# Making the table of q: order of the constants, size of the statistics' parts, and which engine normalises

## The chip, the cores and the metric

The kernel runs on one core of one Trainium2 chip. A core has five engines that each work through their own list of instructions in order and wait for each other through semaphores: PE (matrix products and transposes), DVE (VectorE), ACT (ScalarE), POOL (GpSimd) and SP (SyncE, which here issues DMAs). Sixteen DMA engines move data between the main memory and the core's SBUF. The metric is the device time of one execution in microseconds (us), as the median of several. All times below are us unless they say otherwise.

## What is computed

One layer of a graph network on 12,500 nodes and 212,500 edges, sorted by their target `dst`; a node has 128 features in 8 heads of 16. `x` are the nodes' features, `edge_attr` the edges', and `k`, `v` and `q` are linear maps with weights and biases:

```python
h = jnp.maximum(_layernorm(x), 0.0)
q = (h @ Wq.T + bq).reshape(N, 8, 16)
k = (edge_attr @ Wk.T + bk).reshape(-1, 8, 16)
v = (h @ Wv.T + bv).reshape(N, 8, 16)
qs, qd = q[src], q[dst]
in_m, out_m, diag_m = sum(qs * k), sum(qd * k), sum(qs * qd)   # over the 16 of a head
score = (softmax_by_dst(in_m / 4) + softmax_by_dst(out_m / 4)
         + softmax_by_dst(diag_m / 4)) * weight ** lam
out = segment_sum(score * v[dst], dst) @ Wo.T + bo
return x + leaky_relu(out, 0.1)
```

`_layernorm` subtracts a node's mean over its 128 features and divides by the root of its variance plus 1e-5. The change lies in the first two lines: normalise, cut at zero, multiply by Wq.

## The kernel before, in words

`ordered_path` does the work when `dst` is sorted, which it checks on the way; `general_path` is there for other inputs and is not entered. `ordered_path` has a preparation and then a loop over the edges.

**The preparation** (lines 676 to 984) makes two tables in main memory: `q_table`, q in fp32, one row of 512 bytes a node; and `q3_table`, the same numbers split in three bf16 terms. It also turns the lists of edges. The 12,500 nodes are 98 tiles of 128 nodes, which lie in `xq` [128, 98, 128] in SBUF; four tiles are a group `g`, so there are 25 groups (GN), the last of two tiles. For a group there are these steps:

- `statistics(lo, hi)` (L832 to L847): on DVE one `bn_stats` a tile (L836), then five small operations on a whole part (L841 to L846) that make the sum and the square deviation of each node. Parts are those of the loads of x: 4, 4, 6 and then 14 tiles at a time.
- `scale` (L849 to L854): a root on ACT (L851), a reciprocal (L852) and a product (L853) on DVE, which give each node's factor `inv` and summand `shift`.
- `rectify(g)` (L862 to L865): ACT normalises each of the four tiles in place and cuts at zero in the same pass (L864, 128x128).
- `turn_h(g)` (L867 to L873): PE turns the four tiles into `h_ps` (L871), ACT copies them to `hT` (L873, 128x512).
- `nodes_q(g)` (L875 to L885): PE multiplies by Wq into `q_ps` (L879), DVE adds the bias and writes q over the group's tiles in `xq` (L882), SP writes them to `q_table` (L883).

These are staggered: the loop `for g in range(-2, GN)` issues `rectify(g + 2)`, `turn_h(g + 1)` and `nodes_q(g)`, then `ready` (the scales that will be needed) and `measure` (statistics up to 6 to 12 groups ahead). `h_ps` and `q_ps` have three buffers each.

Beside that loop runs other preparation, hung on it by a table `side` that names a step g: `edges_0` (POOL turns the indices `src_r` and `dst_r` into floats, L778 and L779), `turn_ws` (three weights), `biases`, `edges_1` (PE turns the sources, sixteen transposes into four buffers of `t_ps`, L765, and DVE copies them to `src_i`, L766; then POOL takes differences of neighbours in dst, `step`, L784), `edges_2` (the same turning for the edges' weights into `att_t`) and `edges_3` (POOL makes the segments' borders, L791, DVE makes dst relative, L796, POOL casts it, L799). `t_ps` has two buffers. `step` lies in the memory of `src_r`, so it waits until the sources are turned.

**What sets the order.** Nearly every instruction is passed through `pin`, which chains it behind the one pinned before it on its engine: the program's order is the engine's order. The framework adds the waits for data. The DMAs that SP issues share eight semaphores in turn, so each waits until the eighth before it has landed. SP's list, in order: lam, Wq, the loads of x (ten, L688 and L690), src, weight and dst (L602 to L604), three biases, then sixteen DMAs that pick single indices out of dst (`bases`, `heads`, `tops`, L731 to L738; 83 or 84 numbers of 4 bytes each but the last), then the 25 writes of `q_table` (L883), among them, behind the seventh, three writes of the biases' terms (L828) and, behind the tenth, the fetch of the edges' features of step 0 (`ea`, L643, 1280 KB) and two of single indices, then the borders and relative targets (L803 to L805) and the 25 writes of `q3_table` (L905).

After the loop over g, POOL issues 50 gathers: `gather(0)` to `gather(11)`, four DMAs each, and two for the 20 odd edges (L651, L674). A gather fetches 128 rows of `q_table` by the indices in `src_i`; it needs all of `q_table` written. Beside them ACT and DVE make the terms of q3 (`terms_q`, L896 to L903), with four buffers.

**The loop over edges** (L1377, 415 blocks of 512 edges in 83 steps of five) turns the edges' features, multiplies them by Wk, spreads the targets' q by a one-hot product from `q3_table`, multiplies with the gathered rows, sums over heads, and does the three softmaxes by scans. Its working memory lies where the preparation's was, so its first instructions wait for what used that.

Of the kernel before, what the change touches and what calls it, by code (L numbers as in the profile page):

```python
# [7 lines left out]
F32 = mybir.dt.float32  # L8
# [464 lines left out]
def ordered_path(ctx: ExitStack, tc: tile.TileContext, flag, x, src, dst, edge_attr, edge_weight,  # L473
# [66 lines left out]


    consts = ctx.enter_context(tc.tile_pool(name="consts", bufs=1))
    jp = consts.tile([P, P], I32, name="jp")
    nc.gpsimd.iota(jp, pattern=[[1, P]], base=0, channel_multiplier=-1)
    ident = consts.tile([P, P], F32, name="ident")
    nc.vector.tensor_scalar(ident, jp, 0.0, None, op0=ALU.is_equal)

    third = consts.tile([P, 1], F32, name="third")
    threes = consts.tile([P, W], F32, name="threes")
# [8 lines left out]

    eps = consts.tile([P, 1], F32, name="eps")
    nc.vector.memset(eps, EPS)  # L560
    wq, wv, wk, wo = [consts.tile([P, F], F32, name=n) for n in ("wq", "wv", "wk", "wo")]
# [24 lines left out]
    load = edges.enter_context(tc.tile_pool(name="load", bufs=2))  # L586

    pinned = {}

    def pin(inst):  # L590

        engine = str(inst.ins.engine)
        if engine in pinned:
            tc.add_manual_dep(inst.ins, pinned[engine], mybir.DependencyInfo(
                mybir.DependencyClass.NoSync, mybir.DependencyReason.DATA), reason="in order")
        pinned[engine] = inst.ins.name
        return inst

# [93 lines left out]
    with tc.tile_pool(name="prep", bufs=1) as prep, \  # L692
# [67 lines left out]
        def turn_edges(of, to, which=range(RB)):  # L760
            cols = of.rearrange("r (a p j) -> r a j p", a=RB, j=JN)
            for a in which:
                t_ps = prep_ps.tile([P, JN, RW], F32, name="t_ps")
                for j in range(JN):
                    pin(nc.tensor.transpose(t_ps[:, j, :], cols[:, a, j, :], ident[:RW, :RW]))  # L765
                pin(nc.vector.tensor_copy(to[:, a:NB:RB, :], t_ps.rearrange("p j r -> p r j")))  # L766
# [9 lines left out]
        def edges_0():  # L776

            pin(nc.gpsimd.tensor_copy(src_f, src_r))  # L778
            pin(nc.gpsimd.tensor_copy(dst_f, dst_r))  # L779

        def edges_1():
            turn_edges(src_f, src_i)
            step = got["step"] = prep.tile([RW, RC + 1], F32, name="step", tag="step")
            pin(nc.gpsimd.tensor_sub(step, dst_f[:, 1:], dst_f[:, :RC + 1]))  # L784

        def edges_2():
            turn_edges(weight, att_t)

# [41 lines left out]

        def statistics(lo, hi):

            n = hi - lo
            stats = node.tile([P, CH, 6], F32, name="stats", bufs=1)[:, :n]
            for i in range(n):
                pin(nc.vector.bn_stats(stats[:, i, :], xq[:, lo + i, :]))  # L836


            sums3 = node.tile([P, 3, CH], F32, name="sums3", bufs=4)[:, :, :n]
            total, apart, sq = sums3[:, 0], sums3[:, 1], sums3[:, 2]  # L840
            pin(nc.vector.tensor_add(total, stats[:, :, 1], stats[:, :, 4]))  # L841
            pin(nc.vector.tensor_sub(apart, stats[:, :, 1], stats[:, :, 4]))
            pin(nc.vector.tensor_add(sq, stats[:, :, 2], stats[:, :, 5]))
            pin(nc.vector.scalar_tensor_tensor(apart, apart, F / 4.0, apart, op0=ALU.mult,
                                               op1=ALU.mult))
            pin(nc.vector.tensor_add(sq, sq, apart))  # L846
            return lo, hi, total, sq  # L847
# [14 lines left out]
        def rectify(g):  # L862
            for i in tiles_of(g):
                pin(nc.scalar.activation(xq[:, i, :], xq[:, i, :], AF.Relu, bias=shift[:, i:i + 1],  # L864
                                         scale=inv[:, i:i + 1]))  # L865

        def turn_h(g):  # L867
            n = len(tiles_of(g))
            h_ps = node_ps.tile([P, JN, P], F32, name="h_ps")
            for b, i in enumerate(tiles_of(g)):  # L870
                pin(nc.tensor.transpose(h_ps[:, b, :], xq[:, i, :], ident))  # L871
            hT = hTs[g] = node.tile([P, JN, P], F32, name="hT", bufs=2)
            pin(nc.scalar.copy(hT[:, :n], h_ps[:, :n]))  # L873

# [33 lines left out]

        side = {0: edges_0, 4: turn_ws, 6: biases, 9: edges_1, 15: edges_2, 18: edges_3}
        turn_w(0, wq)  # L910
        parts = [(2 * lo, 2 * hi) for lo, hi in zip(LOADS, LOADS[1:])]

        measured = []

        def measure(upto):

            while parts and parts[0][0] < (upto + 1) * JN:
                measured.append(statistics(*parts.pop(0)))

        def ready(upto):  # L920
# [606 lines left out]
```

## Time and profile before

| what | value |
| --- | --- |
| median of 10 runs | 2692.48 (2686.34 to 2695.48) |
| the profiled execution | 2694.61 |
| its span, first to last instruction | 2692.8 |
| granted PE clock, mean | 0.754 |
| busy in the span: PE, DVE, ACT, POOL | 1773.1, 2001.5, 1342.6, 1644.9 |
| moved by DMA | 351.19 MB, 130 GB/s over the span |

The preparation and the start of the loop in stretches of 10 us, busy time of each engine and what the DMA did:

| us | PE | DVE | ACT | POOL | DMA share | GB/s |
| --- | --- | --- | --- | --- | --- | --- |
| 10 to 20 | 7.19 | 7.53 | 8.01 | 3.70 | 1.10 | 345 |
| 20 to 30 | 8.64 | 8.68 | 8.56 | 0.33 | 1.07 | 263 |
| 30 to 40 | 7.72 | 9.86 | 8.94 | 1.92 | 0.51 | 121 |
| 40 to 50 | 1.69 | 9.76 | 3.11 | 1.90 | 0.07 | 1 |
| 50 to 60 | 9.65 | 4.92 | 7.26 | 7.98 | 0.70 | 232 |
| 60 to 70 | 9.43 | 5.57 | 9.38 | 2.74 | 1.01 | 327 |
| 70 to 80 | 9.13 | 5.51 | 9.66 | 3.94 | 0.45 | 154 |
| 80 to 90 | 1.45 | 8.50 | 4.44 | 5.44 | 0.90 | 277 |
| 100 to 110 | 0.00 | 7.92 | 6.94 | 7.60 | 0.71 | 241 |

How to read it: a span in the profile runs from the first to the last instruction of one execution. A row of the timeline gives the start, the duration, the engine, the line, the operation and its tiles (out<-in); what stands in square brackets is how long the engine had been idle and what ended that. `SPq` rows are the issue of a DMA, not its transfer. A row with xN holds N instructions that followed each other, and its duration is from the first's start to the last's end. In rows of stretches each engine has its busy time and number of instructions, then the granted PE clock, the DMA's share and its GB/s.

### The profile page before, as it was taken

To read this page: it belongs to the slowest core of one execution; us is meant where nothing else is said; L and a number is where in the kernel's file an instruction comes from. 1 tells how busy PE (TensorE), PEld (TensorE's weight loads), DVE (VectorE), ACT (ScalarE), POOL (GpSimd) and SP (SyncE) were. 2 spreads that over 40 slices of the span, in tenths; PEclk is the share of its full clock that TensorE was granted. 3 is DMA by queue.
4 is the path that set the end of the run, shared out by engine and by line. 5 is a ranking of instruction groups with operands and counts; after the bars stand their busy time and mean duration, and the time that the engine had idled before them with its cause. 6 is when DMAs were issued, how large, how long until landed. Compare 5 with 4: busy or idle time off the path is not lost.

```text
span 2692.8 us, 34795 instructions
## 1 busy us (share of the span) xinstructions
PE 1773.1 (66%) x10209; PEld 1430.8 (53%) x10209; DVE 2001.5 (74%) x2582; ACT 1342.6 (50%) x2445; POOL 1644.9 (61%) x1690
## 2 busy tenths in 40 slices
PE   6136665667576676776766677677766676667775
PEld 5135454545465564555655565565555555555654
DVE  7547777777687777777777777787777777778784
ACT  6534444445455454554545455445454555445572
POOL 4656666666666666666666666666666666666610
PEclk9667778777767767787777777766787778777687
DMA  7764334444444444434444444444444444444431
GB/s 206 229 199 136 113 113 132 120 120 114 139 126 123 117 140 132 124 116 146 126 121 124 142 131 119 124 138 131 118 120 141 130 123 123 137 130 125 117 100 52
DMA packets 314459, 351.19 MB, mean 130 GB/s; under 512 B 132882, under 2 KB 234013, under 8 KB 313952
## 3 DMA queue, kind: packets, MB, share of 16 engines
q1 hardware_dynamic: 245493, 233.57, 27.4%
q0 software_dynamic: 53344, 109.11, 16.2%
q10 hardware_dynamic: 15424, 6.19, 0.9%
q8 instruction: 83, 1.36, 0.2%
q14 instruction: 115, 0.94, 0.1%
HBM read 316.50 MB, written 32.17 MB: 129 GB/s over the span
## 4 chain that ended last, share of the span: by engine, by line
PE 26%; ACT 11%; another core or an unknown queue 11%; issue 9%; DVE 9%; DMA 1%; POOL 0%; SPq 0%; DVEq 0%; ACTq 0%; POOLq 0%
PE k_ps L1127 9%; PE w_ps L1274 5%; PE eT_ps L1118 3%; PE qd_ps L1135 3%; ACT eT L1120 2%; DVE u L1202 2%; ACT relb L1112 2%; PE k_ps L1125 2%; ACT qd L1138 2%; ACT sel L1264 1%; ACT oh L1113 1%; DVE prod L1146 1%; ACT sel L1263 1%; DVE prod L1147 1%
## 5 line engine op out<-in xcount | busy, mean ns | idle before, releaser
L651 POOL DMA_INDIRECT qq<-q_table,src_i x1660 | 1609.6, 970 | 883.8 <-issue 359.4
L1127 PE MATMUL k_ps<-wk,eT 128*128 128x128 f32 x3320 | 659.5, 360 | 594.4 <-ACT eT L1120 363.4
L1127 PEld LDWEIGHTS k_ps<-wk,eT 128*128 128x128 f32 x3320 | 559.7, 255 | 750.9 <-ACT eT L1120 420.7
L1149 DVE TENSOR_REDUCE lT<-prod 128x96 f32<-128x1536 f32 x415 | 727.5, 1753 | 14.3
L1120 ACT COPY eT<-eT_ps 128x512 f32<-128x512 f32 x415 | 243.7, 587 | 910.5 <-remote 626.8
L1146 DVE TENSOR_TENSOR prod<-qd,k_ps 128x512 f32<-128x512 f32 x415 | 280.8, 677 | 169.6 <-remote 79.0
L1118 PE MATMUL eT_ps<-ident,ea 128*128 128x128 f32 x1660 | 343.6, 346 | 1.0 <-DVE found L956 1.0
L1135 PE MATMUL qd_ps<-win,oh 126*128 126x128 bf16 x1660 | 190.4, 246 | 199.6 <-DMA q_table<-q 72.1
L1138 ACT COPY qd<-qd_ps 128x512 f32<-128x512 f32 x415 | 239.4, 577 | 125.3 <-remote 32.0
L1112 ACT ACTIVATE relb<-relb,before 126x512 bf16<-126x512 bf16 x415 | 301.6, 727 | 0.0
L1147 DVE TENSOR_TENSOR prod<-qq,qd_ps 128x512 f32<-128x512 f32 x415 | 281.9, 679 | 0.0
L1148 DVE TENSOR_TENSOR prod<-qq,k_ps 128x512 f32<-128x512 f32 x415 | 281.8, 679 | 0.0
L1135 PEld LDWEIGHTS <-oh 126*128 126x128 bf16 x1660 | 148.1, 112 | 250.8 <-issue 168.1
L1113 ACT ACTIVATE oh<-relb 126x512 bf16<-126x512 bf16 x415 | 261.4, 630 | 34.2 <-issue 21.0
L1118 PEld LDWEIGHTS eT_ps<-ident,ea 128*128 128x128 f32 x1660 | 276.0, 184 | 1.3 <-DVE found L956 1.3
L1202 DVE TENSOR_TENSOR_SCAN u<-far,u,l_ps 120x512 f32<-120x512 bf16 x82 | 104.9, 1279 | 230.4 <-remote 57.3
L1274 PE MATMUL w_ps<-back,sel 128*126 128x144 f32 (+1 forms) x1344 | 230.4, 334 | 29.5 <-ACT sel L1264 19.0
L1274 PEld LDWEIGHTS w_ps<-back,sel 128*126 128x126 f32 (+1 forms) x1344 | 212.5, 228 | 54.8 <-ACT sel L1264 43.9
L1125 PE MATMUL k_ps<-b,ones 3*128 3x512 bf16 x415 | 181.4, 437 | 18.9 <-DVE prod L1148 9.4
L1234 DVE TENSOR_TENSOR back<-lT,m_ps 128x480 f32<-128x480 f32 x83 | 54.0, 651 | 145.8 <-PE m_ps L1226 83.8
L1214 DVE TENSOR_TENSOR_SCAN m<-far,head,u 120x512 f32<-120x512 bf16 x83 | 106.4, 1282 | 0.1
L1279 ACT COPY rows<-w_ps 126x288 f32<-126x288 f32 x84 | 33.1, 394 | 122.9 <-PE qd_ps L1135 48.8
(192 smaller groups left out, 1390.9 us busy)
## 6 DMA issues: line engine op xcount, KB each, us to landing
ea<-in_edge_attr_dram SPq DMA_DIRECT2D x83, 1280.0 KB
relb<-rel_d SPq DMA_DIRECT2D x83, 630.0 KB
qq<-q_table,src_i POOLq DMA_INDIRECT x1660
win<-q_table SPq DMA_DIRECT2D x415, 31.5 KB
far<-far_d SPq DMA_DIRECT2D x84, 120.2 KB
q_table<-q SPq DMA_DIRECT2D x24, 384.0 KB
sums<-rows SPq DMA_DIRECT2D x412, 7.9 KB
q_table<-xq SPq DMA_DIRECT2D x24, 256.0 KB
```

The lines of the kernel that those rows point to most:

```text
L651: rows = pin(nc.gpsimd.indirect_dma_start(out=qq[:, j, :], out_offset=None, in_=q_table, in_offset=bass.IndirectOffsetOnAxis(ap=src_i[:, g ...
L1112: pin(nc.scalar.activation(d, d, AF.Abs, bias=before[:K3]))
L1113: pin(nc.scalar.activation(oh, d, AF.Relu, bias=1.0, scale=-1.0))
L1118: pin(nc.tensor.transpose(eT_ps[:, j, :], eas[g // S][:, g % S, j * F:(j + 1) * F], ident))
L1120: pin(nc.scalar.copy(eT, eT_ps))
L1127: pin(nc.tensor.matmul(k_ps[:, j, :], eTs[g][:, j, :], wk, start=False, stop=(j == JN - 1)))
L1135: pin(nc.tensor.matmul(qd_ps[:, j, :], ohs[g][:, j * P:(j + 1) * P], d["win"][:, s, :], start=(j == 0), stop=(j == JN - 1)))
L1138: pin(nc.scalar.copy(qds[g], qd_ps))
L1146: pin(nc.vector.tensor_mul(prod[:, :, 2, :], qds[g], ks[g]))
L1147: pin(nc.vector.tensor_mul(prod[:, :, 1, :], qqs[g], q_ps[g]))
L1149: pin(nc.vector.tensor_reduce(lTs[t][:, :, s, :], prod.rearrange("p j i (h d) -> p j (i h) d", d=DIM), AX.X, ALU.add))
L1274: pin(nc.tensor.matmul(w_ps[:, i].rearrange("p s c -> p (s c)"), d["sel"][:n, j, lo:lo + 3, :].rearrange("p s w -> p (s w)"), d["back"][:n ...
```

## The change

It does five things.

1. The identity matrix, the constant eps and one root of it (`root`, used by nobody) are pinned at the head of DVE's and ACT's lists.
2. The statistics go by parts of 4, 4, 8, 8, ..., 8, 2 tiles. `measure(n)` issues the next n `bn_stats`, whatever parts they lie in: eight before the loop, then six a step. When a part is full its five small operations follow; from tile 16 on they are six and run on POOL.
3. `rectify` no longer cuts at zero: `Relu` moves from the normalisation to the copy of `hT`. In the groups 3 to 11 the fourth tile is normalised by POOL (9 tiles), from group 12 on the third and fourth by DVE (24 tiles); the rest stays on ACT.
4. The table `side` is spread out: the sources' four pieces go at the steps 11, 12, 13 and 14, the weights' two halves at 15 and 16, and `edges_0` moves from step 0 to 9.
5. `measure` is called ahead of `ready` in a step instead of behind it, and `ready` looks three groups ahead instead of four.

The definition of `pin` moves up unchanged. The line numbers of the text are those of the kernel before.

```diff
--- before.py
+++ after.py
@@ -539,12 +539,27 @@
     sums = [dram.tile([NP, 2, 2 * H3], F32, name=f"sums{i}") for i in range(S)]
 
 
...
     consts = ctx.enter_context(tc.tile_pool(name="consts", bufs=1))
     jp = consts.tile([P, P], I32, name="jp")
     nc.gpsimd.iota(jp, pattern=[[1, P]], base=0, channel_multiplier=-1)
     ident = consts.tile([P, P], F32, name="ident")
-    nc.vector.tensor_scalar(ident, jp, 0.0, None, op0=ALU.is_equal)
-
+    pin(nc.vector.tensor_scalar(ident, jp, 0.0, None, op0=ALU.is_equal))
+
+    eps = consts.tile([P, 1], F32, name="eps")
+    pin(nc.vector.memset(eps, EPS))
+    root = consts.tile([P, 1], F32, name="root")
+    pin(nc.scalar.activation(root, eps, AF.Sqrt))
     third = consts.tile([P, 1], F32, name="third")
     threes = consts.tile([P, W], F32, name="threes")
     nc.gpsimd.iota(threes, pattern=[[3, W]], base=0, channel_multiplier=-1,
@@ -556,8 +571,6 @@
     ones3 = consts.tile([3, P], BF, name="ones3")
     nc.vector.memset(ones3, 1.0)
 
-    eps = consts.tile([P, 1], F32, name="eps")
-    nc.vector.memset(eps, EPS)
     wq, wv, wk, wo = [consts.tile([P, F], F32, name=n) for n in ("wq", "wv", "wk", "wo")]
     b3 = consts.tile([3, 3, F], BF, name="b3")
     bv3, bk3, bo3 = [b3[:, i, None, :].to_broadcast([3, JN, F]) for i in range(3)]
@@ -778,13 +780,28 @@
             pin(nc.gpsimd.tensor_copy(src_f, src_r))
             pin(nc.gpsimd.tensor_copy(dst_f, dst_r))
 
+        def turn_src(a):
+            turn_edges(src_f, src_i, [a])
+
         def edges_1():
-            turn_edges(src_f, src_i)
+            turn_src(3)
             step = got["step"] = prep.tile([RW, RC + 1], F32, name="step", tag="step")
             pin(nc.gpsimd.tensor_sub(step, dst_f[:, 1:], dst_f[:, :RC + 1]))
 
+        def edges_1a():
+            turn_src(0)
+
+        def edges_1b():
+            turn_src(1)
+
+        def edges_1c():
+            turn_src(2)
+
         def edges_2():
-            turn_edges(weight, att_t)
+            turn_edges(weight, att_t, (0, 1))
+
+        def edges_2b():
+            turn_edges(weight, att_t, (2, 3))
 
         def edges_3():
             of = got["cuts"] = of_tile()
@@ -828,22 +845,36 @@
                 pin(nc.sync.dma_start(b3[i:i + 1], terms[:, i]))
 
 
-        def statistics(lo, hi):
+        parts = [(0, 4), (4, 8)] + [(lo, min(lo + 8, NI)) for lo in range(8, NI, 8)]
+        waiting = [(lo, hi, i) for lo, hi in parts for i in range(lo, hi)]
+        measured, now = [], {}
+
+        def measure(n):
+
+            for lo, hi, i in waiting[:n]:
+                if i == lo:
+                    now["stats"] = node.tile([P, 8, 6], F32, name="stats", bufs=2)
+                pin(nc.vector.bn_stats(now["stats"][:, i - lo, :], xq[:, i, :]))
+                if i == hi - 1:
+                    measured.append(sum_up(lo, hi, now["stats"][:, :hi - lo]))
+            del waiting[:n]
+
+        def sum_up(lo, hi, stats):
 
             n = hi - lo
-            stats = node.tile([P, CH, 6], F32, name="stats", bufs=1)[:, :n]
-            for i in range(n):
-                pin(nc.vector.bn_stats(stats[:, i, :], xq[:, lo + i, :]))
-
-
-            sums3 = node.tile([P, 3, CH], F32, name="sums3", bufs=4)[:, :, :n]
-            total, apart, sq = sums3[:, 0], sums3[:, 1], sums3[:, 2]
-            pin(nc.vector.tensor_add(total, stats[:, :, 1], stats[:, :, 4]))
-            pin(nc.vector.tensor_sub(apart, stats[:, :, 1], stats[:, :, 4]))
-            pin(nc.vector.tensor_add(sq, stats[:, :, 2], stats[:, :, 5]))
-            pin(nc.vector.scalar_tensor_tensor(apart, apart, F / 4.0, apart, op0=ALU.mult,
-                                               op1=ALU.mult))
-            pin(nc.vector.tensor_add(sq, sq, apart))
+            sums2 = node.tile([P, 2, 8], F32, name="sums2", bufs=5)[:, :, :n]
+            total, sq = sums2[:, 0], sums2[:, 1]
+            apart = node.tile([P, 8], F32, name="apart", bufs=2)[:, :n]
+            of = nc.vector if lo < 16 else nc.gpsimd
+            pin(of.tensor_sub(apart, stats[:, :, 1], stats[:, :, 4]))
+            pin(of.tensor_add(sq, stats[:, :, 2], stats[:, :, 5]))
+            if lo < 16:
+                pin(of.scalar_tensor_tensor(apart, apart, F / 4.0, apart, op0=ALU.mult, op1=ALU.mult))
+            else:
+                pin(of.tensor_mul(apart, apart, apart))
+                pin(of.tensor_scalar(apart, apart, F / 4.0, None, op0=ALU.mult))
+            pin(of.tensor_add(sq, sq, apart))
+            pin(of.tensor_add(total, stats[:, :, 1], stats[:, :, 4]))
             return lo, hi, total, sq
 
         def scale(lo, hi, total, sq):
@@ -861,8 +892,14 @@
 
         def rectify(g):
             for i in tiles_of(g):
-                pin(nc.scalar.activation(xq[:, i, :], xq[:, i, :], AF.Relu, bias=shift[:, i:i + 1],
-                                         scale=inv[:, i:i + 1]))
+                aside = nc.gpsimd if 3 <= g < 12 and i % 4 == 3 else \
+                    nc.vector if g >= 12 and i % 4 > 1 else None
+                if aside:
+                    pin(aside.tensor_scalar(xq[:, i, :], xq[:, i, :], inv[:, i:i + 1],
+                                            shift[:, i:i + 1], op0=ALU.mult, op1=ALU.add))
+                else:
+                    pin(nc.scalar.activation(xq[:, i, :], xq[:, i, :], AF.Identity,
+                                             bias=shift[:, i:i + 1], scale=inv[:, i:i + 1]))
 
         def turn_h(g):
             n = len(tiles_of(g))
@@ -870,7 +907,7 @@
             for b, i in enumerate(tiles_of(g)):
                 pin(nc.tensor.transpose(h_ps[:, b, :], xq[:, i, :], ident))
             hT = hTs[g] = node.tile([P, JN, P], F32, name="hT", bufs=2)
-            pin(nc.scalar.copy(hT[:, :n], h_ps[:, :n]))
+            pin(nc.scalar.activation(hT[:, :n], h_ps[:, :n], AF.Relu))
 
         def nodes_q(g):
             n = len(tiles_of(g))
@@ -906,24 +943,16 @@
                     q3_table[3 * lo:3 * (lo + n * P), :].rearrange("(u p k) f -> p u (k f)", p=P, k=6),
                     q3.rearrange("p (u k) t f -> p u (k t f)", k=2)))
 
-        side = {0: edges_0, 4: turn_ws, 6: biases, 9: edges_1, 15: edges_2, 18: edges_3}
+        side = {4: turn_ws, 7: biases, 9: edges_0, 11: edges_1a, 12: edges_1b, 13: edges_1c, 14: edges_1,
+                15: edges_2, 16: edges_2b, 17: edges_3}
         turn_w(0, wq)
-        parts = [(2 * lo, 2 * hi) for lo, hi in zip(LOADS, LOADS[1:])]
-
-        measured = []
-
-        def measure(upto):
-
-            while parts and parts[0][0] < (upto + 1) * JN:
-                measured.append(statistics(*parts.pop(0)))
-
         def ready(upto):
 
             while measured and measured[0][0] < (upto + 1) * JN:
                 scale(*measured.pop(0))
 
-        measure(1)
-        ready(1)
+        measure(8)
+        ready(0)
         for g in range(-2, GN):
             if g + 2 < GN:
                 rectify(g + 2)
@@ -931,8 +960,8 @@
                 turn_h(g + 1)
             if g >= 0:
                 nodes_q(g)
-            ready(g + 4)
-            measure(g + 6 + min(max(g, 0), 6))
+            measure(6)
+            ready(g + 3)
             if g in side:
                 side[g]()
             if g == 9:
```

More of the change, by code (lines that the diff above doesn't have):

```diff
@@ L539, in ordered_path, with pin @@
     sums = [dram.tile([NP, 2, 2 * H3], F32, name=f"sums{i}") for i in range(S)]
+    pinned = {}
+    def pin(inst):
+        engine = str(inst.ins.engine)
+        if engine in pinned:
+            tc.add_manual_dep(inst.ins, pinned[engine], mybir.DependencyInfo(
+                mybir.DependencyClass.NoSync, mybir.DependencyReason.DATA), reason="in order")
+        pinned[engine] = inst.ins.name
+        return inst
     consts = ctx.enter_context(tc.tile_pool(name="consts", bufs=1))
@@ L586, in ordered_path @@
     load = edges.enter_context(tc.tile_pool(name="load", bufs=2))
[L588 to L597, printed above, removed]
     def rows_in(to, t, q):
```

## The prediction

> **What bounds the kernel now.** I read the page first, for its slices and its chain that ended last, then busy time in stretches of 2 us for the first 90 us, then the timeline of that start, engine by engine, then the rows of SP's queue and of the tile q_table.
>
> ```profile
> span 2692.8 us, 34795 instructions
> ...
> PE 26%; ACT 11%; another core or an unknown queue 11%; issue 9%; DVE 9%; DMA 1%; POOL 0%; SPq 0%; DVEq 0%; ACTq 0%; POOLq 0%
> ```
>
> The chain lies almost wholly in the loop over edges, which begins near 158 us. The change touches only what lies before 84 us, so the question is one shift: how much earlier does the loop begin? Its order on every engine is the same in both kernels. From the timeline of the start:
>
> ```profile
> 34.44 1.88 DVE L843 TENSOR_TENSOR sums<-stats 128x14 f32<-128x14 f32 x1
> ...
> 49.52 0.61 SPq L738 DMA_DIRECT2D tops<-in_dst_dram  x1
> 50.09 1.34 PEld L765 LDWEIGHTS t_ps<-ident,src_r 104*128 104x128 f32 x8 [8.57 <-DVE src_i L766]
> ...
> 51.09 4.26 SPq L883 DMA_DIRECT2D q_table<-xq  x7
> ...
> 52.65 0.58 ACT L873 COPY hT<-h_ps 128x512 f32<-128x512 f32 x1 [9.53 <-PE h_ps L871]
> ...
> 61.01 20.15 SPq L883 DMA_DIRECT2D q_table<-xq  x15
> ...
> 83.65 1.08 POOL L651 DMA_INDIRECT qq<-q_table,src_i  x1 [7.11 <-DMA rel_d<-of]
> ...
> 158.19 0.63 ACT L1113 ACTIVATE oh<-relb 126x512 bf16<-126x512 bf16 x1 [21.02 <-issue]
> ```
>
> Read from below. ACT's first one-hot (L1113) had its input at 137.2 and started at 158.19, 1.5 us after the last of the 50 gathers issued before the loop ended (155.70 + 0.94); it is the first to write memory that the preparation gave back, and the gathers must be out. The gathers (L651) start at 83.65 when the last piece of q_table has landed; POOL had been idle for 7.11. The writes of q_table (L883) follow in two groups; the last is issued at 80.7, as the q stage ends. Inside the stage PE stands 8.57 and ACT 9.53 us: PE wants a t_ps buffer, and DVE reaches the copies of src_i (L766) only at 49.45, behind parts of 14 statistics. But SP issues its first write of q_table only at 51.09, although q of the first group was ready at 18.6: until 50.1 it issues the loads in front, from 37.55 on sixteen of single indices at some 0.76 each. The stretches show what the DMA did meanwhile:
>
> ```profile
> 44.00:46.00 2.00, 0.00 (x0) 0.00 (x0) 2.00 (x4) 0.00 (x0) 0.00 (x0) 0.63 0.08 1
> ...
> 52.00:54.00 2.00, 2.00 (x11) 2.00 (x10) 0.39 (x1) 1.35 (x4) 2.00 (x1) 0.50 1.02 338
> ...
> 60.00:62.00 2.00, 1.80 (x13) 1.20 (x12) 1.06 (x3) 2.00 (x6) 2.00 (x1) 1.00 0.93 229
> ...
> 68.00:70.00 2.00, 1.97 (x17) 1.65 (x16) 1.04 (x4) 2.00 (x7) 0.00 (x0) 1.00 1.09 385
> ...
> 74.00:76.00 2.00, 1.81 (x14) 1.40 (x13) 0.69 (x1) 2.00 (x6) 2.00 (x1) 1.00 0.43 147
> ```
>
> The last two columns are DMA share and GB/s: idle before 51, full from 52 to 56 and from 64 to 70, and paced by the compute after 72.
>
> **The change, part by part.**
>
> *Identity and root table first.* The second ACT_TABLE_LOAD (1.28 at 9.57) goes, and the two masks leave the place between statistics and reciprocals. The second part's sums end at 8.3 as now (its tiles land at 6.79); reciprocal 0.18 and shift 0.16 follow, so the first normalisation starts near 8.7 instead of 11.61: 2.9 us gained on the compute.
>
> *Statistics six a step, parts of 8.* The 98 bn_stats stay (0.20 each back to back). A step costs DVE 6 x 0.20 + the q add 0.60 + half of 0.23 + 0.17 = 2.0 us.
>
> *Sums on POOL from tile 16 on.* Eleven parts of six small operations. The trace has no such row on POOL: below, 0.10 (MEMSET 128x1); above, 1.2 (IOTA 21x840). A tensor_tensor of 2049 columns takes 3.6, so 8 columns are nearest to the low end; I take 0.2, that is 1.2 a part, every second step. DVE now waits for POOL when it is two parts ahead.
>
> *Normalisations.* ACT's step of four and a copy is 2.02 (from 70.83 to 72.85); one activation is 0.39. With three it is 1.63, with two 1.24, plus half a root (0.15). POOL takes 9 tiles: L791 needs 7.12 for 2048 columns, so 0.45 for 128; with overhead 0.5, above it the IOTA's 1.2. DVE takes 24 tiles: L796 gives 0.42 for 512 columns, L552 0.36 for 42; I take 0.2. The ReLU moves into the copy of hT at no charge: an activation of that size is one pass either way, and against the copy's 0.57 the nearest other activation (L1112, 0.73) would add 0.16 a step, under the steps of 2.0.
>
> *Sources in pieces.* The same 16 transposes and four copies (0.54 each), now one a step beside work, so t_ps is free in time: the 9 us hole goes. The casts of src and dst move behind POOL's normalisations, but they waited for data anyway (34.36 and 40.04). Behind the dst cast stand the sums of the last three parts; DVE's last statistics wait for the first of these, near 43.5. Subtraction, cut and cast (3.6 + 7.1 + 3.9) follow on POOL from about 44 and end near 60, before the gathers. SP's order is unchanged except that the bias writes go behind one more write of q.
>
> The sum of the compute: q of group 0 near 15 (it came 6.3 after the first normalisation), two slow steps to 20.5, eleven steps of 2.05 to 43, eleven more of about 1.45 with 3 us for extra transposes: 62; with the wait for dst up to 67. Today it ends at 80.6.
>
> **But that is not what the gathers get.** SP still starts at 51.09. Behind it lie 25 writes, 6.42 MB, and the edges of step 0, 1.31 MB: 7.73 MB. By the rates above: ten writes (2.62 MB) at 338 GB/s take 7.8 us, ending at 59.7; the edges at some 250 take 5.2; the remaining 3.8 MB at 378 take 10. Last byte at 75.0, gathers about 1 us later: 76.0 instead of 83.65, **7.6 us gained**. All at 378 would give 73.4, all at 300 78.7. So compute has some 8 us of slack, and ACT's saved 33 x 0.39 = 12.9 us mostly end in it. The 50 gathers (72 us) and the terms of q3 (they now wait for SP's queue, not the compute) move with it. The loop starts near 150.6. The profiled run took 2694.61, 1.8 beyond its span and 2.1 above the median of ten; it becomes 2687.0, and the median 2692.48 becomes **2684.9**.
>
> *A rule that speaks against it.* L843 took 1.88 instead of 0.17 while POOL cast src (L778, 34.36 to 36.28), so POOL can stop DVE; but L853, at 60.23 inside POOL's tensor_scalar L791, took its usual 0.17, and L882, with one input in PSUM, kept its 0.69. By these rows only the two casts stop DVE, at most 3.8 us, inside the slack. The Trainium skill, SBUF — State Buffer, "Who interferes with whom", says that the shared port pair is an exclusive lock held for the whole instruction, also between a GpSimd operation and a VectorE operation with two SBUF inputs or tensor_scalar in a two-port mode. L843 agrees, L853 does not. By that rule DVE's normalisations could stand behind up to 14.6 us of POOL's three long operations; the compute would end near 77 and the gain would be about 5.
>
> **Rivals.**
> - *The compute's gain comes through whole* (0.07): gathers near 64, some 19 us gained, 2673. The idle DMA until 51 speaks for room; SP's rows until 50.1 and 7.73 MB at no more than 385 GB/s (20 us, so 71 at best) speak against it.
> - *POOL becomes the bound, slower* (0.12). Eleven parts of six operations and nine tiles lie in the way of every scale. If a small operation costs 1.0, the parts take 66 and the tiles 5; with a start near 15 and 8 us for the last steps, q ends at 94 and the gathers start near 97: +13, 2706. It decides from about 0.8 an operation. For it: IOTA 1.2 and the rough spans of POOL. Against it: 0.10 for small MEMSETs, and 0.11 between two dependent operations (L784, L791).
> - *The head start shrinks or is lost* (0.24): the queue runs nearer 300 GB/s, POOL and DVE stop each other, or the gathers, still beside the q3 writes (one took 2.97 at 85.03), go slower: 0 to 5 gained, near 2690.
> - *As computed* (0.57): 5 to 10 gained.
>
> **How the numbers follow.** 0.2% is 5.4 us, about what a measurement can tell here. Faster: the forecast, nearly all of it, and the first rival, 0.63. Same: the third rival, with a small part of the others, 0.26. Slower: the second, 0.11. The range from 2676 to 2693 holds the forecast and most of the third rival and leaves out the first and the second, about 2 in 10; the likeliest case alone is 2682 to 2687.
>
> **What would show it.** Right: one table load, first normalisation near 8.7; no hole of PE from 42 to 50; last q add between 60 and 68; SP's first write of q_table still near 51, then DMA full until about 74; first gather at 75 to 77; first one-hot near 150. Wrong: POOL's small operations near 1 us with DVE waiting for them; SP's writes starting earlier than 51, which would free the rest of the gain; gathers that start earlier and end no earlier; or a loop that takes back what it was given.

## The result, and the profile after

The changed kernel takes **2701.93** (median of 8 runs, 2699.52 to 2703.95) where the kernel before took 2689.34 on the same chip (28 runs): ratio **1.0044**, 95% interval 1.0035 to 1.0053. It is 12.6 slower; 2684.9 was forecast, and the time lies outside the range. Line numbers in the rows below are those of each kernel itself; in the changed one the normalisation is L898 (POOL, DVE) and L901 (ACT), the q add L919, the write of q_table L920, the cut L808.

The page of the changed kernel, span and chain of what ended last:

```profile
span 2704.6 us, 34853 instructions
...
PE 28%; another core or an unknown queue 12%; ACT 11%; DVE 10%; issue 10%; DMA 1%; SPq 0%; DVEq 0%; ACTq 0%
```

The chain is still the loop's, as before. The change touches only what lies ahead of the loop, so the start is where to look first. The changed kernel's timeline of the start, the rows that answer to those shown of before:

```profile
8.56 1.65 ACT L901 ACTIVATE xq<-xq,shift,inv 128x128 f32<-128x128 f32 x4 [2.33 <-DVE shift L884]
...
48.45 0.74 SPq L740 DMA_DIRECT2D tops<-in_dst_dram  x1
48.57 0.62 PE L767 MATMUL t_ps<-ident,src_r 104*128 104x104 f32 x4
...
50.13 5.06 SPq L920 DMA_DIRECT2D q_table<-xq  x8
...
60.94 32.64 SPq L920 DMA_DIRECT2D q_table<-xq  x15
...
96.08 1.11 POOL L653 DMA_INDIRECT qq<-q_table,src_i  x1 [13.73 <-DMA rel_d<-of]
...
146.59 0.63 ACT L1142 ACTIVATE oh<-relb 126x512 bf16<-126x512 bf16 x1 [5.53 <-issue]
```

The beginning is as forecast: first normalisation at 8.56 instead of 11.61, transposes of the sources without a wait, SP's first write of q_table at 50.13. Then it goes wrong: the last fifteen writes take 32.64 to issue, because q isn't there, and the gathers start at 96.08 instead of 83.65 (12.4 later; 76.0 was forecast). The stretches show what the DMA did meanwhile (the columns as before; the last two are DMA share and GB/s):

```profile
52.00:54.00 2.00, 1.03 (x7) 0.67 (x7) 1.97 (x9) 1.19 (x3) 0.92 (x5) 1.00 1.03 344
...
74.00:76.00 2.00, 2.00 (x14) 2.00 (x14) 0.55 (x2) 0.65 (x2) 0.00 (x0) 0.67 0.01 2
```

Full at first, the DMAs stand still from 74 to 76: the table waits for the compute, not the compute for the table. The timeline of DVE, POOL and ACT shows what the compute stood for:

```profile
48.48 1.89 POOL L781 CAST dst_r<-dst_r 104x2050 f32<-104x2050 int32 x1 [0.34 <-DMA bases<-in_dst_dram]
48.87 1.84 DVE L898 TENSOR_SCALAR xq<-xq,inv,shift 128x128 f32<-128x128 f32 x2
...
57.88 0.59 DVE L898 TENSOR_SCALAR xq<-xq,inv,shift 128x128 f32<-128x128 f32 x2
58.39 3.60 POOL L789 TENSOR_TENSOR step<-dst_r 104x2049 f32<-104x2049 f32 x1 [0.55 <-PE t_ps L767]
59.49 9.79 DVE L898 TENSOR_SCALAR xq<-xq,inv,shift 128x128 f32<-128x128 f32 x2
62.08 7.12 POOL L808 TENSOR_SCALAR of<-step 104x2048 bf16<-104x2048 f32 x1
66.61 2.68 DVE L919 TENSOR_TENSOR xq<-q_ps,bq_all 128x512 f32<-128x512 f32 x1
69.57 0.88 ACT L901 ACTIVATE xq<-xq,shift,inv 128x128 f32<-128x128 f32 x2 [9.27 <-DVE shift L884]
...
78.31 4.13 DVE L898 TENSOR_SCALAR xq<-xq,inv,shift 128x128 f32<-128x128 f32 x2
78.47 3.88 POOL L816 CAST of<-dst_r 104x2048 bf16<-104x2048 f32 x1 [9.27 <-DVE dst_r L813]
```

Two of DVE's new normalisations usually take 0.59. Beside POOL's cast of dst they take 1.84, beside its subtraction and cut 9.79, beside its last cast 4.13, and each pair ends with POOL's instruction or one normalisation behind it (9.79 from 59.49 ends at 69.28, the cut at 69.20; 4.13 from 78.31 at 82.44, the cast at 82.35). That is 1.25 + 9.20 + 3.54 = 14.0 more; the q add, the reciprocal and the shift queue behind, and ACT stands 9.27. Against the kernel before this is where the lead turns into a loss: the 14th of the 25 q adds still comes 2.5 earlier (56.48 against 59.02), the 16th 3.4 later (66.61 against 63.18). That is the first theory: **POOL's long instructions stop DVE's normalisations.** The rivals are a broken chain (scales issued too late: ACT waits 1.2 to 4.4 for DVE's shift every second step, also before 50), another place in memory, and the two parts that end in a wait for something else.

### The profile page after: what moved, and what is told of

Read it like the earlier page. It is cut to its first block, busy times and chain, and to the rows that moved or that the text cites. A ratio compares the mean times of both kernels' runs of the same rounds, so it can differ in the third digit from the quotient of the medians.

```text
span 2704.6 us, 34853 instructions
## 1 busy us (share of the span) xinstructions
PE 1769.7 (65%) x10209; PEld 1434.0 (53%) x10209; DVE 2018.8 (75%) x2586; ACT 1328.7 (49%) x2417; POOL 1671.7 (62%) x1765
## 4 chain that ended last, share of the span: by engine, by line
PE 28%; another core or an unknown queue 12%; ACT 11%; DVE 10%; issue 10%; DMA 1%; SPq 0%; DVEq 0%; ACTq 0%
PE k_ps L1156 9%; PE w_ps L1303 6%; PE eT_ps L1147 4%; PE qd_ps L1164 3%; DVE u L1231 2%; ACT eT L1149 2%; PE k_ps L1154 2%; DVE prod L1176 2%; ACT relb L1141 2%; ACT sel L1293 2%; DVE prod L1175 2%; ACT sel L1292 2%; ACT qd L1167 2%; ACT oh L1142 1%
## 5 line engine op out<-in xcount | busy, mean ns | idle before, releaser
L1303 PE MATMUL w_ps<-back,sel 128*126 128x144 f32 (+1 forms) x1344 | 244.2, 348 | 27.2 <-ACT sel L1293 18.2
L1303 PEld LDWEIGHTS w_ps<-back,sel 128*126 128x126 f32 (+1 forms) x1344 | 225.3, 241 | 54.8 <-ACT sel L1293 49.2
```

What stands on the lines that cost most here:

```text
L1303: pin(nc.tensor.matmul(w_ps[:, i].rearrange("p s c -> p (s c)"), d["sel"][:n, j, lo:lo + 3, :].rearrange("p s w -> p (s w)"), d["back"][:n ...
```

## The experiments

They ran on several chips, each beside runs of the kernel before on the same chip (medians 2269.31, 2668.16, 2691.12 and 2268.39), so ratios are compared; the changed kernel itself ran only beside the result. Starts in the first 100 us can be compared directly: e4, the kernel before but for one unused constant, has its first gather at 83.33 on another chip, against 83.65. "Last q add" is the start of the last row of q adds.

| kernel | last q add | first gather | ratio, 95% interval |
| --- | --- | --- | --- |
| before | 79.57 | 83.65 | 1 |
| changed | 91.96 | 96.08 | 1.0044 (1.0035 to 1.0053) |
| e1 DVE normalises nothing | 82.19 | 86.31 | 1.0013 (1.0002 to 1.0024) |
| e2 scales early | 90.47 | 94.56 | 1.0038 (1.0025 to 1.0051) |
| e3 both | 80.17 | 84.25 | 1.0013 (1.0003 to 1.0022) |
| e4 before, other place | 79.85 | 83.33 | 0.999 (0.9979 to 1.0001) |
| e5 e3, biases at 19 | 82.48 | 86.56 | 1.0011 (1.0003 to 1.002) |
| e6 e5, index loads late | 75.45 | 79.53 | 1.0021 (1.0012 to 1.0029) |
| e7 changed, cut on DVE | 82.95 | 87.06 | 1.0011 (1.0002 to 1.0021) |
| e8 before, pieces | 72.52 | 76.98 | 0.9984 (0.9975 to 0.9992) |
| e9 e8, identity first | 73.5 | 78.95 | 0.9985 (0.9975 to 0.9994) |
| e10 e8, index loads late | 74.8 | 78.87 | 1.0016 (1.0005 to 1.0027) |
| e11 e5, cut on DVE | 75.12 | 79.21 | 0.9998 (0.9987 to 1.001) |
| e12 e9, cut on DVE | 73.61 | 78.11 | 0.9991 (0.9982 to 1.0001) |
| e13 e9, biases after q | 78.75 | 83.09 | 0.9994 (0.9983 to 1.0005) |
| e14 e13, index loads between writes | 67.06 | 74.37 | 0.9965 (0.9951 to 0.9978) |

In all but e9 and e14 the first gather comes 3.5 to 4.6 after the start of the last row of q adds: there the compute decides it. And but for e6 and e10 the time follows the first gather to within 2.8 (changed: 12.4 later, 12.6 slower; e8: 6.7 earlier, 5.1 faster; e14: 9.3 earlier, 8.7 faster).

Why it follows is shown on two of the chips only. The gathers' rows on the pages of e4 and of the kernel before (busy time, mean ns of one, then POOL's idle time before them):

```profile
L653 POOL DMA_INDIRECT qq<-q_table,src_i x1660 | 1612.1, 971 | 512.7 <-issue 300.1
...
L651 POOL DMA_INDIRECT qq<-q_table,src_i x1660 | 1609.6, 970 | 883.8 <-issue 359.4
```

In e4 the idle time is 0.31 a gather, the usual distance between two, and so it is in e1 to e3, e13 and e14 (513 to 519), which ran on the chips with medians near 2269: POOL issues one gather after the other to the end of the loop, so a later first gather moves them all. On the other chips, that of the result among them, the idle time is 844 to 888, so there POOL also waits for others, and the path from the first gather to the end isn't shown: of the 12.4 the changed kernel's loop is 0.9 behind at its 21st one-hot (273.96 against 273.04), 11.3 at the 201st (1355.77 against 1344.43) and 12.8 at the last.

**e1, e2, e3: the stopped normalisations or the late scales.** e1 and e3 give DVE's tiles back to ACT, e2 and e3 add a `ready`:

```diff
-                aside = nc.gpsimd if 3 <= g < 12 and i % 4 == 3 else \
-                    nc.vector if g >= 12 and i % 4 > 1 else None
+                aside = nc.gpsimd if 3 <= g < 12 and i % 4 == 3 else None
```
```diff
+            ready(g + 4)
             measure(6)
             ready(g + 3)
```

> The changed kernel, but ACT normalises the third and fourth tile from group 12 on, so DVE normalises none. Theory of the blocked port: in the changed kernel's trace DVE's normalisations took 9.79 us (59.49, until POOL's L808 ended), 4.13 (78.31, until POOL's cast L816 ended) and 1.84 (48.87, the dst cast) where others of the same kind take 0.59; these 14 us go, ACT's steps grow to 2.2, the last q add moves from 92.5 to about 78 and the first gather from 96.1 to about 81; time about 2690. Theory of the scale chain alone (DVE's reciprocal stands behind six statistics and a product of PE): no change of the first 50 us, and with ACT loaded again the end of q stays beyond 88 and the time above 2697. Theory of the loop (6 us of the loss arise after the start): the time gains what the gathers gain, the rest stays.

> The changed kernel, but the scales are issued ahead of a step's statistics and one group earlier (ready(g + 4), then measure(6), then ready(g + 3) for the first parts). Theory of the scale chain: ACT's waits of 1.2 to 4.4 us for the product of DVE at every second step go, group 11's q add comes near 42 instead of 50.6, the last near 82 to 84 since the blocked port (14 us) stays; time about 2692. Theory of the blocked port alone: the first 50 us keep their pace, end of q still beyond 90, time above 2699.

> Both edits together: no normalisation on DVE, and early scales. Expected if port and chain explain the late end of q: the last q add between 66 and 72, then SP and the DMA bind as predicted: first write of q_table near 50, DMA full until about 75, first gather at 76 to 78, 6 to 8 us before that of the kernel before (83.65); time about 2682 to 2685. If the loop takes something back or the loss lies in the loop, the gathers come at 76 to 78 and the time is 2687 or more.

e1 takes 9.8 off the first gather, and some three quarters of the loss are gone (3.1 us are left of 12.6, on another chip); e2 takes off 1.5. The stops are the large term. But e3 stays at 84.25: as e1 it missed what the sum without stops promised. In e3 the early scales win 2.2 by the eighth q add (33.94 for 36.10) and lose them at the next: DVE stands 3.86 for the load of the biases, which step 7 wants. And POOL still stops other operations of DVE (below).

**e4: place in memory.**

```diff
     ident = consts.tile([P, P], F32, name="ident")
+    spare = consts.tile([P, 1], F32, name="spare")
+    nc.vector.memset(spare, 0.0)
```

> The kernel before with one more constant of 4 bytes a partition, never used, which moves every tile behind it by 32 bytes, as the changed kernel does. Theory that the place in memory slows the loop (the changed kernel's loop falls back from 5.7 us late at its third block to 12 at its last): 4 to 6 us slower, 2694. Theory that only the preparation matters: no difference, 2689 within 2.

The interval leaves no room for 4 to 6 us: this shift of the tiles is no cause.

**e7: the stop alone.** DVE keeps its normalisations; only the cut changes its engine.

```diff
-            pin(nc.gpsimd.tensor_scalar(of, got["step"][:, :RC], 0.0, -FAR, op0=ALU.is_gt, op1=ALU.mult))
+            pin(nc.vector.tensor_scalar(of, got["step"][:, :RC], 0.0, -FAR, op0=ALU.is_gt, op1=ALU.mult))
```

> The changed kernel with one instruction given to another engine: the cut of POOL's steps to 0 and -FAR (L808, 2048 columns, 7.12 us on POOL) is done by DVE. All else, DVE's normalisations among it, stays. Theory 'POOL's long instructions stop DVE's normalisations': the normalisation that took 9.79 us takes at most about 4 (what is left under the subtraction L789), DVE pays 1 to 2.5 us for the cut; the first gather comes 5 to 8 us before the changed kernel's 96.08, at 88 to 91, ratio about 1.001 to 1.002 where the changed kernel stands at 1.0044. Rival 'those 9.79 us are a wait for data or for another engine that the record puts there': the stretch stays, the gather comes at 96 to 98, ratio 1.004 to 1.005.

The timeline of e7, POOL and DVE:

```profile
57.08 3.61 POOL L789 TENSOR_TENSOR step<-dst_r 104x2049 f32<-104x2049 f32 x1 [0.54 <-PE t_ps L767]
58.19 2.82 DVE L898 TENSOR_SCALAR xq<-xq,inv,shift 128x128 f32<-128x128 f32 x2
...
62.84 0.59 DVE L898 TENSOR_SCALAR xq<-xq,inv,shift 128x128 f32<-128x128 f32 x2
66.37 1.22 DVE L808 TENSOR_SCALAR of<-step 104x2048 bf16<-104x2048 f32 x1
69.29 4.13 DVE L898 TENSOR_SCALAR xq<-xq,inv,shift 128x128 f32<-128x128 f32 x2
69.45 3.88 POOL L816 CAST of<-dst_r 104x2048 bf16<-104x2048 f32 x1 [8.77 <-DVE dst_r L813]
```

With the cut gone from POOL the 9.79 become 2.82, which end 0.3 behind the subtraction; where POOL is idle, 0.59; beside the last cast again 4.13. The gather comes 9.0 earlier, and the ratio is the 1.001 that was forecast. That POOL's cut stops the normalisations is shown, by a change that leaves them where they are; through which part of the chip it does so the traces don't say.

**e5, e6, e11: what else stands in the changed kernel.** e5 is e3 with the biases at step 19; e6 has besides SP's sixteen index loads moved to between the writes of the terms of q; e11 is e5 with the cut on DVE.

```diff
-        side = {4: turn_ws, 7: biases, 9: edges_0, 11: edges_1a, 12: edges_1b, 13: edges_1c, 14: edges_1,
+        side = {4: turn_ws, 19: biases, 9: edges_0, 11: edges_1a, 12: edges_1b, 13: edges_1c, 14: edges_1,
```

> The changed kernel with DVE normalising nothing, with the scales of four more groups allowed ahead, and with the biases of step 7 moved to step 19. In the run with the first two edits DVE stood 3.86 us at step 7 for the load of the biases and the last q add ended near 81, the first gather started at 84.25 and the ratio to the kernel before was 1.0013. Theory 'the stage is stopped by waits that were put into it, the biases' among them': those 3.86 us go, the 12th q add (50 there) comes near 45, the last near 76, the first gather near 79, and the time falls by about 5 us, to a ratio of 0.998 to 0.999. Rival 'the pace is ACT's, four tiles a step at 2.02 us, and the wait was slack': last q add still 79 to 81, gather 83 to 85, ratio 1.001.

> The same with SP's sixteen loads of single indices (0.76 us of issue each) taken from before the writes of q_table to between later writes of q. Theory 'SP starts to write q_table only when these are issued, and this floor of about 75 us stands behind the compute': SP's first write moves from 50 to about 38, but the gathers gain only what the compute leaves, 0 to 3 us on the run with the biases moved; ratio 0.997 to 0.999. Rival 'the compute is the only bound now': first write earlier and the first gather within 1 us of that run's.

> The changed kernel with everything found so far taken out at once: DVE normalises nothing, the scales of four more groups are allowed ahead, the biases come at step 19, and the cut is made by DVE. In the run with the first three PE stood 10.46 us, since the branch over the weights' power stood on POOL behind the cut of 7.12 us. Theory 'waits were what lost, and these were the large ones': the hole of PE near 52 to 62 shrinks to under 4 us, last q add near 73 to 76, first gather 77 to 80, ratio 0.9985 to 1.0005. Rival 'the statistics in sixes with sums on POOL hold the pace by themselves': first gather 83 or later, ratio 1.001 or more.

e5 missed. The 12th q add comes at 44.81 instead of 49.97, so the wait was no slack; then a new one takes it all. The timeline of e5, POOL and PE:

```profile
55.06 7.12 POOL L808 TENSOR_SCALAR of<-step 104x2048 bf16<-104x2048 f32 x1
...
62.29 1.66 PE L767 MATMUL t_ps<-ident,weight 104*128 104x104 f32 x8 [10.46 <-POOLq L747]
```

The weights' power (L747) is a branch that isn't pinned. In e5 POOL meets it behind the cut, and PE's transposes of the weights wait 10.46 for it. In e11, where POOL has no cut, PE waits 3.25 there and the gather comes at 79.21; the time is that of before. So what e11 keeps of the statistics in sixes and the sums on POOL brought no gain: e9, without them, has 78.95, although it stands 3.55 for the biases (below), which e11 doesn't. What they cost by themselves isn't shown.

e6 starts its writes at 36.76 and its gathers 7.0 earlier than e5, against both of its theories. Those 7 come with the compute, not from SP: in e6 POOL meets the branch at 43.22, ahead of the cut, PE waits 1.24 for it, and the last q add comes at 75.45. And e6 isn't faster. e10 tests that.

**e8, e9, e12: the parts of the change on the kernel before.** e8 turns the sources and weights in pieces and keeps all else:

```diff
-        side = {0: edges_0, 4: turn_ws, 6: biases, 9: edges_1, 15: edges_2, 18: edges_3}
+        side = {0: edges_0, 4: turn_ws, 6: biases, 11: lambda: turn_src(0), 12: lambda: turn_src(1),
+                13: lambda: turn_src(2), 14: edges_1, 15: edges_2, 16: edges_2b, 17: edges_3}
```

e9 has the change's first hunk besides (identity, eps and root pinned first); e12 is e9 with the cut on DVE.

> The kernel before with one part of the change alone: sources and weights are turned in pieces, at steps 11 to 16 (edges_3 at 17). Statistics, sums and normalisations stay as they were. Theory 'this part is the sound one: it removes the stop of 8.57 us of PE and 9.53 of ACT behind 14 statistics': the stop goes, the last q add comes 4 to 6 us before 80.6, the first gather at 77 to 80 instead of 83.65, ratio 0.997 to 0.9985. Rival 'SP's queue is the floor': last q add at 75 but the gather not before 80, ratio 0.9985 to 1. Rival 'the transposes only stop elsewhere': gather 83 to 85, ratio 1.

> The kernel before with two parts of the change: sources and weights in pieces, and identity and root table first. Statistics of 14 and their sums on DVE, all normalisations on ACT, as before. With the pieces alone the first gather came at 76.98 and the ratio was 0.9984. Theory 'these two parts are the gain of the change and its other three the loss': first normalisation near 8.7, and the 2.9 us come through in part, since ACT and PE are the pace late in the stage: last q add 70 to 73, first gather 74 to 76.5, ratio 0.997 to 0.9985. Rival 'the table's 2.9 us end in the waits for DVE's blocks of 14 statistics': first normalisation at 8.7, all else within 1 us of the run with the pieces alone.

> The kernel before with the pieces, identity and root table first, and the cut made by DVE. With the pieces alone DVE's copy of the bases (L799, usually about 0.16) took 2.67 us and a shift 1.12 beside POOL's long operations. Theory 'each long POOL operation costs DVE what it stops, and DVE does the cut in 1.2 us': these stops go, DVE pays 1.2 to 2.4, the first gather comes 0 to 2 us before that of the run without the cut, at 73 to 76, ratio 0.996 to 0.998. Rival 'SP's start at 50 is the floor now': first gather stays at that of the run without the cut, ratio within 0.0005 of it.

e8 is faster than both kernels: the stops of 8.57 and 9.53 are gone, the gather comes at 76.98. In e9 the first normalisation starts at 8.75, and the gather no earlier (2.0 later than in e8; SP's first write is 1.6 later); the rival was right that the head start is lost, and the wait is not the one it named. DVE's timeline in e9:

```profile
37.06 0.17 DVE L855 TENSOR_TENSOR sums<-sums 128x14 f32<-128x14 f32 x1
40.78 1.69 DVE L832 CAST terms<-b_row 1x384 bf16<-1x384 f32 x1 [3.55 <-DMA b_row<-in_L_gnn_bo_dram]
```

The biases again: DVE's wait for them ends at 39.4 in the changed kernel, 39.7 in e3 and 40.8 in e9, and 2.9 of head start end there. (Their first cast takes 1.69 instead of 0.35 beside POOL's cast of dst.) In e12 DVE's copy of the bases falls from e8's 2.67 to 0.17 and DVE pays 1.22 for the cut; the gather gains 0.8, the time nothing that can be measured (0.9991, where 0.996 to 0.998 was expected).

**e10: index loads among the terms.** The loops that load `bases`, `heads` and `tops` move from before the loop over g into the loop of `terms_q`:

```diff
             terms_q(g)
+            if g == 2:
+                bases_in()
+            if 5 <= g < 15:
+                (heads_in if g % 2 else tops_in)((g - 5) // 2)
```

> The kernel before with the pieces, and with SP's sixteen loads of single indices moved from before the writes of q_table to between the writes of the terms of q. The run of the changed kernel with the same move had its first gather at 79.53, 7 us before the run without it (86.56), and yet was not faster (1.0021 against 1.0011). Theory 'these loads, put among the writes of the terms, delay the start of the loop': first write of q_table near 36 and first gather within 2 us of 77, but a ratio 0.0005 to 0.0025 above the 0.9984 of the pieces alone. Rival 'the move costs nothing, the difference was something else': ratio 0.997 to 0.9985.

The move costs 0.003 against e8 and against e9, more than the 0.0025 at most that was expected. SP's rows of e9, which keeps the loads in front, and of e10:

```profile
85.34 37.72 SPq L914 DMA_DIRECT2D q_table<-q  x22
126.73 1.42 SPq L640 DMA_DIRECT2D win<-q_table  x2
```
```profile
130.64 26.66 SPq L920 DMA_DIRECT2D q_table<-q  x11
159.31 2.51 SPq L637 DMA_DIRECT2D win<-q_table  x5
```

The writes of the terms end at 157.3 instead of 123.1, and the loop's first windows (`win`) are read from 159.31 instead of 126.73, on the same chip; POOL stands 14.96 ahead of the gather at 167.80, in e9 5.03 ahead of that at 157.95. So the loop of e10 starts late, as the theory said. That this is the whole cost isn't shown: in the kernel before the windows are read from 161.46 (another chip), and it is faster than e10. And it doesn't explain e6, whose windows start at 139.20, ahead of e5's (147.53): there the cause stays open.

**e13, e14: the wait for the biases and SP's start.** e13 is e9 with the biases made in the loop of `terms_q` after g = 5; in e14 one index load goes behind each of the first fifteen writes of q_table (`index_in` holds the three kinds of loads, one a call). The first and the last edit are e13's, the middle one is e14's.

```diff
-        side = {0: edges_0, 4: turn_ws, 6: biases, 11: lambda: turn_src(0), 12: lambda: turn_src(1),
+        side = {0: edges_0, 4: turn_ws, 11: lambda: turn_src(0), 12: lambda: turn_src(1),
...
+            if 0 <= g < 3 * S:
+                index_in(g)
             ready(g + 4)
...
+            if g == 5:
+                biases()
```

> The kernel before with the pieces and the identity and root table first, and the biases' terms made after the fifth step of the terms of q instead of at step 6. Without the last edit the early table gave nothing: DVE stood 3.55 us for the load of the biases (and the first cast took 1.69 beside POOL's cast), and the first gather came at 78.95. Theory 'the head start ends in this wait': the wait goes, the 7th q add comes near 37 instead of 43.9, the last near 69 to 71, the first gather at 74.5 to 77, limited by SP's start at 50 to 51; ratio 0.997 to 0.9985. Rival 'another wait stands right behind it (statistics of 14, the cast of dst, the branch on POOL behind the cut)': first gather 78 to 80, ratio 0.9985 or more.

> The same, with SP's sixteen loads of single indices put one behind each of the writes of q_table, which SP has to wait for anyway; among the writes of the terms they made the time 0.003 longer. Theory 'the place among the terms was the cost, and SP's start at 50 is a floor once the compute is early': first write near 37, first gather with the compute at 73 to 75.5, terms of q as early as in the run without the move, ratio 0.996 to 0.998. Rival 'behind each write they stop the next write': last write later than 2 us after the last q add, gather 77 or later, ratio as in the run without the move or above.

In e13 the wait goes (the q adds that began at 43.94 in e9 begin at 38.46) and, as the rival said, another wait stands behind it: the branch falls behind the cut on POOL (55.57), PE stands 9.32 for it, and the gather comes at 83.09. In e14 POOL meets the branch at 34.87, before the cast of dst, and SP's first write comes at 38.48 instead of 50.05. Its SP and POOL rows:

```profile
38.48 0.40 SPq L898 DMA_DIRECT2D q_table<-xq  x1
...
64.61 6.51 SPq L898 DMA_DIRECT2D q_table<-xq  x10
...
74.37 1.23 POOL L654 DMA_INDIRECT qq<-q_table,src_i  x1 [7.68 <-DMA qq<-in_edge_attr_dram]
```

q is finished near 68, 12 before the kernel before; the gathers follow at 74.37, and the time is 0.9965 of it, the best here. The last write is issued 3 behind the end of the q adds, so SP holds the table back a little, as the rival feared. Since the branch moves too, e14 against e13 doesn't measure the index loads alone.

## Why the prediction was wrong

- **The step that failed** is "by these rows only the two casts stop DVE, at most 3.8 us, inside the slack". The row it rested on, L853 with 0.17 inside POOL's cut, is a scalar_tensor_tensor; the operation that the change adds is a tensor_scalar, and for it the trace of before had no row beside a long POOL instruction. It was stopped for 14.0. The Trainium skill's rule, in SBUF — State Buffer, "Who interferes with whom", was held against that row and set aside; it names tensor_scalar (in a two-port mode; the traces don't say whether this one ran in it), and on it the rule held, with 9.79 beside the cut. On L853 it didn't in that row; in e8, e9 and e14 the same shift takes 1.12, 1.15 and 1.57 inside the cut, so not even for its own pair was one row enough.
- "Compute has some 8 us of slack" failed too, and not by the stops alone. It came from a q stage that ends at 62 to 67; the measured one ends at 93. The eleven steps "of 2.05 to 43" took 3.23 each in the changed kernel (20.99 to 56.48), so it was 13.5 behind the forecast before the long stops began. e11, without DVE's normalisations, ends at 75 to 76, and in e5 the steps took 2.57 (21.36 to 49.62). DVE's busy time was summed, and the waits of ACT for the shift and of DVE for the biases were not. What of the half microsecond a step in e5 belongs to which wait was not taken apart. A normalisation on DVE, taken at 0.2, took 0.3.
- "Identity and root table first: 2.9 gained on the compute" was right at its row (8.56, 8.7 forecast) and wrong as a gain: in e9 it ends in the load of the biases (3.55; 1.13 of that wait stands in the changed kernel).
- "The 9 us hole goes" was right, and alone it is worth 6.7 at the gathers and 0.0016 of the time (e8).
- "SP still starts at 51" was right (50.13). That it bounds the gathers at 76.0 was not tested by the changed kernel; e8 reaches 76.98 with it and e14 74.37 without it.
- Sums on POOL at 0.2 were right: 0.20 to 0.23 each, a normalisation 0.45. The rival that ends slower, 2706 with gathers near 97, comes near the measured 2701.93 and 96.08 by chance: its mechanism, 1.0 a small operation, isn't there. The third rival did name POOL and DVE stopping each other, and expected 0 to 5 gained of it.
- "The gathers must be out" before the first one-hot was a misreading. The row at 155.70 is the 54th gather, not the 50th (150.74), and in the changed kernel the first one-hot ran at 146.59, before the 50th gather (164.43) and 11.6 earlier than in the kernel before, though the gathers start later. So "the loop starts near 150.6" was no sign of the time, and that the time followed the start of the gathers all the same is shown as a mechanism only on the chips of e1 to e4, e13 and e14.

## What to carry to other kernels

Before an operation goes to an engine, list what stands beside it on its neighbour: a row of another kind of operation says little of it, nor does a single row of the same kind, and of POOL instructions of 2 to 7 us the whole length may be the price. A gain at the head of an ordered list is worth what lies before the next event that doesn't move with it, here a load that lands near 40; look for that event and for the one behind it. Test parts of a change singly: of the five here only one was run by itself, and it was sound; with the early constants, the biases and the index loads moved it gave 0.9965.

## What the runs showed of the hardware

POOL doesn't stop every operation of DVE. In e1, POOL's cut runs from 61.41 to 68.53; DVE's timeline:

```profile
65.81 0.20 DVE L883 RECIPROCAL inv<-inv 128x8 f32<-128x8 f32 x1 [0.30 <-ACT inv L882]
66.05 0.17 DVE L884 SCALAR_TENSOR_TENSOR shift<-sums,inv 128x8 f32<-128x8 f32 x1
66.16 2.40 DVE L810 COPY base_c<-dst_r 104x4 f32<-104x4 f32 x1
```

Reciprocal and shift pass at their usual length, and the copy of 4 columns ends with POOL's instruction. Inside the same cut of POOL in e14 (53.71 to 60.83) the shift is slower, though it ends well before the cut:

```profile
56.70 1.57 DVE L868 SCALAR_TENSOR_TENSOR shift<-sums,inv 128x14 f32<-128x14 f32 x1
```

In e12, where POOL has no cut, it takes 0.17 again. The shift takes 3.45 in e5 beside POOL's subtraction (51.37 to 54.97) and 2.58 in e1 beside its last cast: how long DVE stands depends on both operations. POOL takes 7.12 for the cut of 2048 columns, and DVE 1.22.
